# Two graph layers on one core: the product of two weight matrices moved to the front of the program, and the first batches planned anew

## The chip, the cores and the metric

The kernel runs on one core of a Trainium2 chip. The metric is the device time of one execution, in microseconds (us). The engines of a core are TensorE (PE, with its weight loads as PEld), VectorE (DVE), ScalarE (ACT), GpSimd (POOL) and SyncE (SP, which here only issues transfers). [...]

## The reference

There are 32 batches of a 512 x 512 matrix x, one 512 x 512 matrix adj for all of them, and weights of 512 x 512, all in float32. What is computed is this:

```
h = relu(layernorm(x))
x = x + (adj @ h) @ w0 + b0                     # layer 0
h = relu(layernorm(x))
q, k, v = h @ Wq + bq, h @ Wk + bk, h @ Wv + bv  # layer 1, 8 heads
scores = q @ k.T / 8 + (1 - adj) * -1e9
x = x + (softmax(scores) @ v) @ Wo + bo
```

The term with -1e9 makes the softmax of layer 1 pick, for each row of adj, the column with the largest entry, wherever that entry leads by enough. Then layer 1 is a gather of rows of h @ (Wv @ Wo) plus a constant row.

## The kernel before

**Front.** `gnn_two_layers` loads adj, x of batches 0 and 1, Wq, Wk and w0. It transposes adj on PE (L89) into `adjT` (copies at L104), makes the layer norm of batch 0 (`Norm`, with the power on POOL at L201 and the relu on ACT at L212), and multiplies it by adj (L139, called the aggregation; the result, transposed, is `yT`). Beside this DVE looks for the largest entry of each row of adj (L115 to L117), and PE counts which columns are used at all (`few`, L147, and `many`, L137 and L138). From these and from the sums of squares of Wq and Wk it makes a flag that says whether the gather is valid (L164, L165). All engines load the flag (L176) and branch. With these inputs they go to `single_path`; `general_path` is the full attention.

**The single path.** Its order is written by hand. For each batch number b, `todo` holds lists of functions for 21 steps; `put` files a function under a step. Three generators carry the PE work, and with each of their pieces one step's list is run before the piece's result is taken from PSUM. Steps 0 to 6 go with layer 0 of batch b, steps 7 to 13 with the aggregation of batch b+1, steps 14 to 20 with layer 1 of batch b-1. A 512 x 512 product is done in 7 pieces instead of 8 (`product`, matmuls at L288): p1, p5, u2, c11, c22, c12, c21. They use sums of blocks of both operands that DVE makes beforehand (`sum_a`, `sum_b`: `h0s`, `yTs` in the tile `sel`, `adjT_s`, `w0_t`, `wvo_t`, `hTs`). p1, u2, c22 and c21 accumulate in one bank, p5 and c12 in a second one, c11 in a third; a piece in a bank can begin only when the piece before it in that bank has been taken. Takes are copies on ACT or additions on DVE (L325, L327, L335, L338, L345).

**Batch 0.** It has no layer 1 of an earlier batch beside it. Layer 0 of batch 0 is done in plain rows (`layer0_rows`, L458), with DVE making the four `adjT_s` sums beside it. The aggregation of batch 1 follows; at its step 11 `number_rows` (L404 to L414) numbers the used rows with two small PE matmuls and ten small DVE operations, and the four `w0_t` sums are made. In place of layer 1, steps 14 to 20 run `fold_weights`: it transposes Wv (L364, copied by ACT at L365), multiplies it by Wo (L372, copied into `wvo` at L375), and sums the rows of bv-weighted Wo (`part`, made by `bias_part`; matmul L378) into the constant row `cvo` and its column form `cvo_c` (L381 to L385). wv, wo, bv and bo are loaded behind the branch (L587 to L589), ahead of the x of batch 2.

**Later batches.** `put_h` writes h of layer 1 by an indirect DMA in the order of the numbering, `get_h` fetches the used rows, `transpose_h` and `hT_sum` prepare them, layer 1 multiplies by `wvo`, and `finish` adds the gathered rows to x. For the last batch, layer 0 takes its pieces in the order p1, p5, u2, c22, c11, c12, c21, because no layer 1 lies between its aggregation and it.

Of the kernel before, what the change touches and what calls it, by code (L numbers as in the profile page):

```python
# [17 lines left out]
P = 128  # L18
# [7 lines left out]
def gnn_two_layers(ctx: ExitStack, tc: tile.TileContext, x, adj, w0, b0, wq, bq, wk, bk, wv, bv, wo, bo, out):  # L26
# [22 lines left out]
    def big(name):  # L49
# [3 lines left out]
    adjT, yT, w0_s, sel = big("adjT"), big("yT"), big("w0_s"), big("sel")  # L53
    wv_s, wo_s = xs[3], xs[4]
    b0_r = keep.tile([P, D], F32, name="b0_r")
# [7 lines left out]
    kept = dict(xs=xs, hs=hs, adjT=adjT, yT=yT, w0_s=w0_s, sel=sel, wv_s=wv_s, wo_s=wo_s, b0_r=b0_r, used=used,  # L63
                before=before, idx=idx, ident=ident, ones=ones, mhalf=mhalf)
# [3 lines left out]
    with ExitStack() as tmp, tc.manual_schedule():  # L68
# [4 lines left out]
        for c in range(C):  # L73
            nc.sync.dma_start(mask[:, c, :], adj[c * P:(c + 1) * P, :])
            nc.scalar.dma_start(xs[0][:, c, :], x[0, c * P:(c + 1) * P, :])
# [3 lines left out]
        wt = [look.tile([P, DC, D], F32, name=f"wt{i}") for i in range(2)]  # L79
        bt = [look.tile([P, DC], F32, name=f"bt{i}") for i in range(2)]  # L80

        def load_w(t, w):
            nc.scalar.dma_start(t, w.rearrange("(c p) o -> p c o", p=P))

        norms = [Norm(nc, small, mhalf, xs[0], hs[0], [0, 1]), Norm(nc, small, mhalf, xs[0], hs[0], [2, 3])]
        pts = [ps_l.tile([P, C, P], F32, name=f"pt{m}") for m in range(C)]
        for c in range(C):
            for m in range(C):
                nc.tensor.transpose(pts[m][:, c, :], mask[:, c, m * P:(m + 1) * P], ident)  # L89
            norms[c // 2].stats(c % 2)  # L90
            if c == 1:
                norms[0].power()
            if c == 2:
                norms[0].offset()
        norms[1].power()
        for t, v in zip(bt, (bq, bk)):
            nc.gpsimd.dma_start(t, v.rearrange("(c p) -> p c", p=P))
        nc.gpsimd.dma_start(b0_r, bass.AP(tensor=b0.tensor, offset=b0.offset, ap=[[0, P], [1, D]]))
        for i, w in enumerate((wq, wk)):
            norms[0].relu(i)  # L100
            load_w(wt[i], w)
        for m in range(C):
            eng = (nc.scalar.copy, nc.scalar.copy, nc.vector.tensor_copy, nc.vector.tensor_copy)[m]
            eng(adjT[:, m, :], pts[m].rearrange("p c q -> p (c q)"))  # L104
        norms[1].offset()
        for i in range(2):
            norms[1].relu(i)
        if B > 1:
            load_w(xs[1], x[1])
        load_w(w0_s, w0)  # L110

        sums = look.tile([P, 4], F32, name="sums")
        top = look.tile([P, C, 8], F32, name="top")
        for c in range(C):
            nc.vector.tensor_scalar(mask[:, c, :], mask[:, c, :], 1.0, NEG, op0=ALU.subtract, op1=ALU.mult)  # L115
            nc.vector.max(top[:, c, :], mask[:, c, :])
            nc.vector.tensor_scalar(sel[:, c, :], mask[:, c, :], top[:, c, 0:1], None, op0=ALU.is_equal)  # L117
        both = look.tile([P, N], F32, name="both")
# [6 lines left out]
        nc.vector.tensor_reduce(least, gap, AX.X, ALU.min)  # L125

        if B > 1:
            norms.append(Norm(nc, small, mhalf, xs[1], hs[1], range(C)))
            norms[2].stats(0)
            norms[2].stats(1)  # L130
        few = ps_l.tile([P, 4, C], F32, name="few")
        many = ps_l.tile([P, 4, C], F32, name="many")
        for d in range(DC):
            ps = ps_l.tile([P, N], F32, name="mm", bufs=2)
            for m in range(C):
                if d == 3 and m == 2:
                    nc.tensor.matmul(many[:, 0, :], ones, used, start=True, stop=True)  # L137
                    nc.tensor.matmul(many[:, 1, :], ones, sums, start=True, stop=True)  # L138
                nc.tensor.matmul(ps, hs[0][:, m, d * P:(d + 1) * P], adjT[:, m, :], start=(m == 0), stop=(m == C - 1))  # L139
# [5 lines left out]
            if d == 2:  # L145
# [3 lines left out]
                if B > 1:  # L149
                    norms[2].stats(2)  # L150
                    norms[2].stats(3)
                    norms[2].power()
        rows = look.tile([P, 1], F32, name="rows")
        nc.vector.tensor_reduce(rows, many[:, 0, :], AX.X, ALU.add)
        nc.vector.tensor_scalar(rows, rows, float(32 * S), None, op0=ALU.is_le)
# [7 lines left out]
        nc.vector.tensor_mul(sure, sure, rows)  # L163
        nc.tensor.matmul(few[0:1, 1, 0:1], sure, ones[:, 0:1], start=True, stop=True)  # L164
        nc.vector.tensor_copy(flag, few[0:1, 1, 0:1])  # L165
        if B > 1:
            norms[2].offset()
            for c in range(C):
                norms[2].relu(c)
# [9 lines left out]
    with cmp.Else():  # L179
        general_path(tc, x, adj, wq, bq, wk, bk, wv, bv, wo, bo, out, kept)  # L180

# [35 lines left out]
def single_path(ctx: ExitStack, tc: tile.TileContext, x, wv, bv, wo, bo, out, kept):  # L217
# [20 lines left out]
    xs, hs, adjT, yT, w0_s, sel, wv_s, wo_s, b0_r, used, before, idx, ident, ones, mhalf = (  # L238
        kept[k] for k in ("xs", "hs", "adjT", "yT", "w0_s", "sel", "wv_s", "wo_s", "b0_r", "used", "before", "idx",
                          "ident", "ones", "mhalf"))  # L240
# [15 lines left out]

    def blk(t, chunks, cols, half=HALF):
        return t[:, 2 * chunks:2 * chunks + 2, cols * half:(cols + 1) * half]

# [10 lines left out]

    def sum_b(s, t, i, half=HALF):
        b11, b12, b21, b22 = blk(t, 0, 0, half), blk(t, 0, 1, half), blk(t, 1, 0, half), blk(t, 1, 1, half)
        if i == 0:
            nc.vector.tensor_sub(s[:, 0], b12, b11)
        elif i == 1:
            nc.vector.tensor_sub(s[:, 1], b22, s[:, 0])
        elif i == 2:
            nc.vector.tensor_sub(s[:, 2], b22, b12)
        else:
            nc.vector.tensor_sub(s[:, 3], b21, s[:, 1])  # L280
# [68 lines left out]
    adjT_s, w0_t, wvo_t = (consts.tile([P, 4, 2, HALF], F32, name=n) for n in ("adjT_s", "w0_t", "wvo_t"))  # L349
    wvo = consts.tile([P, DC, D], F32, name="wvo")  # L350
    cvo = consts.tile([P, D], F32, name="cvo")
    cvo_c = consts.tile([P, DC], F32, name="cvo_c")
    bv_c = consts.tile([P, DC], F32, name="bv_c")
# [4 lines left out]
    wvT = work.tile([P, DC, D], F32, name="zs")  # L358

    def fold_weights():  # L360
        for j in range(DC):
            pt = ps_t.tile([P, DC, P], F32, name="pt")
            for i in range(DC):
                nc.tensor.transpose(pt[:, i, :], wv_s[:, i, j * P:(j + 1) * P], ident)  # L364
            nc.scalar.copy(wvT[:, j, :], pt.rearrange("p c q -> p (c q)"))  # L365
            if j % 2 == 1:
                for f in (yield) or ():
                    f()
        for i in range(DC):
            ps = ps_m.tile([P, D], F32, name="mm")  # L370
            for j in range(DC):
                nc.tensor.matmul(ps, wvT[:, j, i * P:(i + 1) * P], wo_s[:, j, :], start=(j == 0), stop=(j == DC - 1))  # L372
            for f in (yield) or ():
                f()
            nc.scalar.copy(wvo[:, i, :].rearrange("p (c q e) -> p q c e", q=4, c=4),  # L375
                           ps.rearrange("p (q c e) -> p q c e", q=4, c=4))
        ps = ps_m.tile([P, D], F32, name="mm")
        nc.tensor.matmul(ps, ones, part, start=True, stop=True)  # L378
        for f in (yield) or ():
            f()  # L380
# [5 lines left out]

    part = work.tile([P, D], F32, name="part")

    def bias_part(j):
        if j == 0:  # L390
# [556 lines left out]
```

## Time and profile before

| what | us |
|---|---|
| median of 3 runs | 1108.0 (1107.43 to 1109.12) |
| the profiled execution | 1104.05 |
| its span | 1101.6 |

The profile of one execution shows each engine's instructions with start and length. For a reader of this change the stages ahead of the third batch matter. This is how they lie in the profiled execution, read from PE's instructions in order of time:

| stage | PE from, to (us) |
|---|---|
| transposes of adj, as it comes in | 4.37 to 9.6 |
| aggregation of batch 0, counts, flag | 10.95 to 28.3 |
| layer 0 of batch 0, in rows | 29.63 to 43.44 |
| aggregation of batch 1, with the numbering | 43.44 to 57.35 |
| weights: transposes, product, sum of rows | 57.35 to 74.25 |
| layer 0 of batch 1 | 74.25 to 86.58 |
| aggregation of batch 2 | 86.58 to 98.67 |
| layer 1 of batch 0 | 98.67 to 107.31 |

In the lines of the trace, the columns are start, length (of the group, when several instructions are merged into a line), engine, source line, operation, output and inputs, shape, count, and in brackets the idle time of the engine before it with what ended it. A float32 matmul is carried out as two instructions, so 16 matmuls are shown as x32; a transpose is one instruction.

### The profile page before, as it was taken

How to read it: one execution, taken by the hardware profiler on the slowest of the kernel's cores; microseconds unless marked ns; L12 is line 12 of the kernel's file. 1: busy time of each engine (PE TensorE's matmuls, PEld its weight loads, DVE VectorE, ACT ScalarE, POOL GpSimd, SP SyncE). 2: the span in 40 equal slices, each digit the busy share in tenths (PEclk: the TensorE clock that was granted, in tenths of full speed). 3: DMA queues.
4: the chain of work that ended last, by engine and by line, in shares of the span. 5: the costliest groups of instructions: out<-in, count | busy, mean ns of one | idle time of the engine just before them, and what ended most of it. 6: DMA issues, size and time to landing. Idle time of an engine off the chain costs nothing.

```text
span 1101.6 us, 15852 instructions
## 1 busy us (share of the span) xinstructions
PE 1079.9 (98%) x5404; PEld 953.2 (87%) x5404; DVE 907.3 (82%) x1853; ACT 358.6 (33%) x655; POOL 443.8 (40%) x491
## 2 busy tenths in 40 slices
PE   7999999999999999999999999999999999999996
PEld 3569989999989989988999998999999899999883
DVE  6869888888888888878888888888888878888863
ACT  3223323233323333322323332323332232333221
POOL 2124544333554343454333454433355434345413
PEclk9999999999999999999999999999999999999999
DMA  6362676667777667767666776666776766676537
GB/s 238 125 141 74 172 191 148 160 175 197 182 181 158 149 171 193 187 171 169 157 156 189 193 189 177 146 160 173 196 179 181 164 149 171 184 193 155 141 105 245
DMA packets 162412, 186.90 MB, mean 170 GB/s; under 512 B 14993, under 2 KB 102289, under 8 KB 162321
## 3 DMA queue, kind: packets, MB, share of 16 engines
q1 hardware_dynamic: 130672, 112.70, 37.3%
q0 software_dynamic: 27968, 66.61, 27.0%
q10 hardware_dynamic: 3680, 6.49, 1.7%
q8 instruction: 44, 0.72, 0.3%
q14 instruction: 48, 0.39, 0.2%
HBM read 96.28 MB, written 89.46 MB: 169 GB/s over the span
## 4 chain that ended last, share of the span: by engine, by line
PE 94%; DMA 1%; DVE 1%; ACT 1%; POOL 1%; issue 1%; ACTq 0%; SPq 0%; POOLq 0%; DVEq 0%
PE mm L288 89%; PE mm L139 1%; PE mm L458 1%; PE mm L372 1%; PE mm L508 1%; POOL x L544 1%; DMA x<-in_x_dram 1%; DMA yT<-z,place 1%; ACT h L212 0%; DMA z<-zr 0%; DVE x L345 0%; DVE st L194 0%; ACT zs L338 0%; POOL yT L553 0%; DVE zr L535 0%
## 5 line engine op out<-in xcount | busy, mean ns | idle before, releaser
L544 POOL DMA_INDIRECT x<-z,place x116 | 182.8, 1576 | 370.6 <-DMA z<-zr 318.7
L327 ACT COPY yT<-mm 128x512 f32<-128x512 f32 x124 | 71.8, 579 | 562.0 <-PE mm L288 527.9
L345 DVE TENSOR_TENSOR x<-mm,x 128x512 f32<-128x512 f32 x217 | 149.7, 690 | 86.2 <-PE mm L288 86.2
L212 ACT ACTIVATE h<-x,off,rstd 128x512 f32<-128x512 f32 x256 | 194.9, 808 | 36.2 <-DVE off L204 34.2
L201 POOL TENSOR_TENSOR rstd<-ve,mhalf 128x2 f32<-128x2 f32 (+1 forms) x97 | 106.0, 1093 | 222.1 <-DVE ve L200 222.1
L194 DVE BATCH_NORM_STATS2 st<-x 128x6 f32<-128x512 f32 x256 | 171.5, 670 | 9.2 <-DMA x<-in_x_dram 8.0
L288 PE MATMUL mm<-w_t,sel 128*128 128x256 f32 x744 | 171.1, 380 | 0.8 <-DVE x L345 0.8
L288 PE MATMUL mm<-adjT_s,h0s 128*128 128x256 f32 x744 | 170.8, 380 | 1.0 <-ACT yT L327 1.0
L288 PEld LDWEIGHTS mm<-w_t,sel 128*128 128x128 f32 x744 | 141.5, 191 | 20.4 <-DVE x L345 1.6
L288 PEld LDWEIGHTS mm<-adjT_s,h0s 128*128 128x128 f32 x744 | 141.6, 191 | 20.2 <-ACT yT L327 1.4
L470 POOL DMA_INDIRECT hs<-h,dest x124 | 133.7, 1078 | 30.8 <-issue 22.2
L338 ACT ACTIVATE zs<-mm,cvo_c 128x176 f32<-128x176 f32 x248 | 87.2, 403 | 98.2 <-PE mm L288 98.2
L288 PE MATMUL mm<-hTs,wvo_t 128*128 128x176 f32 x720 | 117.5, 313 | 0.6 <-ACT zs L338 0.6
L288 PE MATMUL mm<-adjT,h 128*128 128x256 f32 x496 | 117.2, 380 | 0.0
L288 PE MATMUL mm<-w_s,yT 128*128 128x256 f32 x496 | 117.2, 380 | 0.0
L288 PEld LDWEIGHTS mm<-hTs,wvo_t 128*128 128x128 f32 x720 | 109.8, 191 | 1.1 <-ACT zs L338 1.1
L288 PEld LDWEIGHTS mm<-adjT,h 128*128 128x128 f32 x496 | 94.5, 191 | 13.0 <-issue 0.5
L288 PEld LDWEIGHTS mm<-w_s,yT 128*128 128x128 f32 x496 | 93.3, 191 | 11.5 <-issue 0.5
L436 DVE TENSOR_TENSOR x<-x,b_r 128x512 f32<-128x512 f32 x128 | 86.6, 678 | 0.0
L288 PE MATMUL mm<-hT,wvo 128*128 128x176 f32 x480 | 81.4, 313 | 0.0
L288 PEld LDWEIGHTS mm<-hT,wvo 128*128 128x128 f32 x480 | 75.3, 190 | 1.5
L325 DVE TENSOR_TENSOR yT<-mm,yT 128x512 f32<-128x512 f32 x93 | 63.9, 687 | 5.8 <-PE mm L288 3.0
(146 smaller groups left out, 1278.9 us busy)
## 6 DMA issues: line engine op xcount, KB each, us to landing
out_dram<-x SPq DMA_DIRECT2D x124, 256.0 KB, 4.1
x<-in_x_dram SPq DMA_DIRECT2D x120, 256.0 KB, 5.5
hc<-hs SPq DMA_DIRECT2D x124, 176.0 KB, 3.8
z<-zr SPq DMA_DIRECT2D x120, 96.0 KB, 2.0
z<-zr SPq DMA_DIRECT2D x120, 80.0 KB, 1.9
hs<-h,dest POOLq DMA_INDIRECT x124, 5.9
x<-z,place POOLq DMA_INDIRECT x116, 5.8
x<-in_x_dram ACTq DMA_DIRECT2D x4, 256.0 KB, 5.3
```

Of the source, the lines that this page charges most:

```text
L139: nc.tensor.matmul(ps, hs[0][:, m, d * P:(d + 1) * P], adjT[:, m, :], start=(m == 0), stop=(m == C - 1))
L194: self.nc.vector.bn_stats(st, self.src[:, self.chunks[i], :])
L201: self.nc.gpsimd.tensor_tensor(self.rstd, ve, self.mhalf[:, 0:n], ALU.pow)
L212: self.nc.scalar.activation(dst, src, AF.Relu, bias=self.off[:, i:i + 1], scale=self.rstd[:, i:i + 1])
L288: nc.tensor.matmul(bank[:, m, 0:half], lhs[:, k, m * P:(m + 1) * P], rhs[:, k, :], start=(first and m == 0 and k == 0), stop=(k == 1), ski ...
L325: nc.vector.tensor_add(dst, bank, dst)
L327: nc.scalar.copy(dst, bank)
L338: nc.scalar.activation(dst[:, m, :], bank[:, m, :], AF.Identity, bias=cvo_c[:, 2 * i + m:2 * i + m + 1])
L345: nc.vector.tensor_add(dst, bank, dst)
L436: nc.vector.tensor_add(X[b][:, c, :], X[b][:, c, :], b0_r)
L470: stored = nc.gpsimd.indirect_dma_start(out=HS[b], out_offset=bass.IndirectOffsetOnAxis(ap=dest[:, i:i + 1], axis=0), in_=H1[b][:, i, :], ...
L544: nc.gpsimd.indirect_dma_start(out=X[b][:, c, :], out_offset=None, in_=Z[b], in_offset=bass.IndirectOffsetOnAxis(ap=place[:, c:c + 1], axi ...
```

## The change

The product Wv @ Wo moves from batch 0 of the single path to the very front, and everything that hangs on it is rearranged:

- wv and wo are loaded first (wv in two halves, one each on the queues of SP and ACT; wo in four chunks in turn). adj, x of batch 0, Wq, Wk, w0 and x of batch 1 follow on SP. bv, bq, bk and b0 are loaded by POOL at once. ACT runs a small relu before its first copy.
- The front then transposes Wv, makes the product and `part`, and transposes adj between the first rows of the product. The search of the largest entries (`peaks`) and the norm of batch 0 stand beside it.
- The four `adjT_s` sums are made ahead of the aggregation of batch 0 and the four `w0_t` sums within it, both ahead of the branch. The relu of batch 1 is ahead of the flag too.
- `few` comes after the second of the aggregation's four rows instead of the third, `many` one matmul earlier.
- In batch 0 of the single path, `number_rows` is at step 1, the statistics of layer 1 at steps 2, 3 and 7, `put_h` at 9 and 11, `get_h` at 16, the norm of batch 2 at 8 to 14. The weights' steps fall away: layer 0 of batch 1 follows its aggregation directly, with its pieces in the order of the last batch.
- What is left of the weights (the matmul with `part` and the constant row: `add_up`) goes to step 11 of batch number 1, beside the aggregation of batch 2. The `wvo_t` sums go from steps 4, 4, 5, 5 to 5, 5, 6, 6.
- `general_path` keeps its Wq, Wk and h in the new tiles; it does not run with these inputs.

The diff, cut to its core:

```diff
-        for c in range(C):
-            nc.sync.dma_start(mask[:, c, :], adj[c * P:(c + 1) * P, :])
-            nc.scalar.dma_start(xs[0][:, c, :], x[0, c * P:(c + 1) * P, :])
+        nc.sync.dma_start(wv_s[:, 0:2, :], rows(wv, 0, 2))
+        nc.scalar.dma_start(wv_s[:, 2:4, :], rows(wv, 2, 2))
+        for c in range(DC):
+            (nc.sync, nc.scalar)[c % 2].dma_start(wo_s[:, c:c + 1, :], rows(wo, c, 1))
+        for t, w in ((mask, adj), (xs[0], x[0])):
+            for c in (0, 2):
+                nc.sync.dma_start(t[:, c:c + 2, :], rows(w, c, 2))
+        for t, w in [(wt[0], wq), (wt[1], wk), (w0_s, w0)] + [(xs[1], x[1])] * (B > 1):
+            nc.sync.dma_start(t, rows(w, 0, C))
...
+        for t, v in ((bv_c, bv), (bt[0], bq), (bt[1], bk)):
             nc.gpsimd.dma_start(t, v.rearrange("(c p) -> p c", p=P))
...
+        nc.scalar.activation(first, ones[:, 0:1], AF.Relu)
+
+        def transposed(t, dst, engines):
+            pts = [ps_l.tile([P, C, P], F32, name=f"pt{m}") for m in range(C)]
+            for c in range(C):
+                for m in range(C):
+                    nc.tensor.transpose(pts[m][:, c, :], t[:, c, m * P:(m + 1) * P], ident)
+                if c % 2 == 1:
+                    yield
+            for m in range(C):
+                engines[m](dst[:, m, :], pts[m].rearrange("p c q -> p (c q)"))
+            yield
...
+        for _ in transposed(wv_s, wvT, (nc.scalar.copy, nc.scalar.copy, nc.vector.tensor_copy, nc.vector.tensor_copy)):
+            pass
+        for j in range(DC):
...
+                nc.vector.scalar_tensor_tensor(part, wo_s[:, j, :], bv_c[:, j:j + 1], part, op0=ALU.mult, op1=ALU.add)
+        flips = transposed(mask, adjT, (nc.scalar.copy,) * 4)
+        for i in range(DC):
+            ps = ps_l.tile([P, D], F32, name="mm", bufs=2)
+            for j in range(DC):
+                nc.tensor.matmul(ps, wvT[:, j, i * P:(i + 1) * P], wo_s[:, j, :], start=(j == 0), stop=(j == DC - 1))
+            if i == 0:
+                next(flips)
+                peaks(0)
+                peaks(1)
+            if i == 1:
+                next(flips)
...
+            nc.scalar.copy(wvo[:, i, :].rearrange("p (c q e) -> p q c e", q=4, c=4),
+                           ps.rearrange("p (q c e) -> p q c e", q=4, c=4))
...
+        for i in range(4):
+            sum_b(nc, adjT_s, adjT, i)
...
-                if d == 3 and m == 2:
+                if d == 3 and m == 1:
                     nc.tensor.matmul(many[:, 0, :], ones, used, start=True, stop=True)
...
-            if d == 2:
+            if d == 1:
                 for m in range(C):
                     nc.tensor.matmul(few[:, 0, m:m + 1], both[:, m * P:(m + 1) * P], ones[:, 0:1], start=True, stop=True)
                 nc.vector.tensor_scalar_min(used, few[:, 0, :], 1.0)
...
+                    for c in range(C):
+                        norms[2].stats(c)
                     norms[2].power()
...
+                for i in range(4):
+                    sum_b(nc, w0_t, w0_s, i)
+                if B > 1:
+                    norms[2].offset()
+            if d == 2 and B > 1:
+                for c in range(C):
+                    norms[2].relu(c)
...
-        for t, w in ((wv_s, wv), (wo_s, wo)):
-            nc.sync.dma_start(t, w.rearrange("(c p) o -> p c o", p=P))
...
     def layer0(b):
-        if b == B - 1:
+        if b in (1, B - 1):
             return product(yT, yTs, w0_s, w0_t, take_onto(X[b]), pieces=("p1", "p5", "u2", "c22", "c11", "c12", "c21"))
...
+            if b == 0:
+                put(0, 1, lambda b: number_rows())
+                todo[3] += todo[4] + todo[5] + todo[6]
+                run(layer0_rows(0), todo[0:4])
...
+                put(1, 11, lambda b: add_up())
...
-            if b == 0:
-                run(fold_weights(), todo[14:21])
-            else:
-                run(layer1(b - 1) if b < B and b != B - 2 else None, todo[14:21])
+            run(layer1(b - 1) if 0 < b < B and b != B - 2 else None, todo[14:21])
```

`add_up` is the end of `fold_weights` (L378 to L385), unchanged. `sum_b` is the function of the same name in the single path, moved out of it.

## Prediction

> **What bounds the kernel now.** I read the page first: the engines' busy time, the slices and the chain that ended last.
>
> ```profile
> PE 1079.9 (98%) x5404; PEld 953.2 (87%) x5404; DVE 907.3 (82%) x1853; ACT 358.6 (33%) x655; POOL 443.8 (40%) x491
> PE   7999999999999999999999999999999999999996
> PE 94%; DMA 1%; DVE 1%; ACT 1%; POOL 1%; issue 1%; ACTq 0%; SPq 0%; POOLq 0%; DVEq 0%
> ```
>
> TensorE (PE) has work in every slice and carries 94% of the chain. So only three things can move the time: when PE starts, what it waits for, and how fast it is clocked. The edits touch the front and batches 0 and 1. From layer 0 of batch 2 on (107.31 us, the first L288 `w_s,yT` matmul after layer 1 of batch 0) the plan is the same but for the batch number in conditions. I therefore compare what lies ahead of 107.31. Next I read PE and its weight loads in order of time.
>
> ```profile
> 4.37 2.24 PE L89 MATMUL pt<-ident,mask 128*128 128x128 f32 x8 [4.37 <-DMA mask<-in_adj_dram]
> 8.50 1.12 PE L89 MATMUL pt<-ident,mask 128*128 128x128 f32 x4 [0.17 <-DMA mask<-in_adj_dram]
> 10.95 12.50 PE L139 MATMUL mm<-adjT,h 128*128 128x512 f32 x24 [1.33 <-ACT adjT L104]
> ...
> 13.67 0.34 PEld L139 LDWEIGHTS mm<-adjT,h 128*128 128x128 f32 x1 [0.52 <-issue]
> 14.52 0.34 PEld L139 LDWEIGHTS mm<-adjT,h 128*128 128x128 f32 x1 [0.52 <-issue]
> 15.13 0.19 PEld L139 LDWEIGHTS mm<-adjT,h 128*128 128x128 f32 x1 [0.27 <-issue]
> 15.56 0.19 PEld L139 LDWEIGHTS mm<-adjT,h 128*128 128x128 f32 x1 [0.24 <-issue]
> ```
>
> Dense work starts at 10.95. Its loads step by 0.85 us until about 14.95 and by 0.43 us afterwards: 4.0 us at half rate, 2.0 us lost. The page's PEclk row reads 9 throughout, so the spacing is the evidence. Then what PE waits for later, in order of time, and one row of the table by stage (busy us of PE, weight loads, DVE, ACT, POOL; clock; DMA):
>
> ```profile
> 55.52 2.00 PE L288 MATMUL mm<-adjT_s,h 128*128 128x256 f32 x8 [1.11 <-DVE yT L325]
> 57.35 1.04 PE L364 MATMUL pt<-ident,x 128*128 128x128 f32 x8
> 58.68 1.15 PE L364 MATMUL pt<-ident,x 128*128 128x128 f32 x8 [0.29 <-ACT zs L365]
> 59.66 13.90 PE L372 MATMUL mm<-x,zs 128*128 128x512 f32 x32
> 73.39 1.02 PE L378 MATMUL mm<-part,ones 128*128 128x512 f32 x2
> ...
> 1050.60 2.00 PE L288 MATMUL mm<-w_t,sel 128*128 128x256 f32 x8 [0.78 <-DVE x L345]
> ...
> 98.67:107.31 8.64, 8.63 (x58) 8.36 (x57) 8.54 (x20) 5.49 (x11) 3.85 (x4) 1.00 0.43 86
> ```
>
> The first row is `number_rows`: its VectorE (DVE) chain sat ahead of c22's take, and c21 accumulates in the bank that take reads. The row at 1050.60 is the one layer 0 that already runs in the order p1, p5, u2, c22. In the last row the third busy figure is DVE: 8.54 of 8.64 us in layer 1 of batch 0, no slack.
>
> **The change, part by part.**
>
> *Start of dense work.* Before, four adj and four x loads of 256 KB come in side by side; the fourth of the eight lands at 5.64, the last at about 8.8. Then relu and the adjT copies lead to 10.95. Now wv comes first, two 512 KB loads on two queues: the same first megabyte, so 5.6. Sixteen transposes at 0.28 (2.24 for 8) end at 10.1. The first copy (0.57, ACT) starts when its bank is done, three transposes earlier, and is over by then; wo, the second megabyte, is in by 8.8. The product starts at 10.1: **-0.85**. ACT's table load (1.28) is called early and leaves the path. Four ACT-queue issues of 0.39 to 0.52 (L83) go to SP, which has nothing else to do. The bias loads take 0.8 to 1.2 each of POOL from 1.6 on and land 6.5 to 7.6 after issue, so bv is there by 9.5; DVE wants it at 11.1.
>
> *Transposes.* Those of wv leave 57.35 to 59.66 (2.31 with the 0.29 wait); those of adj now stand between products at 16 x 0.13 = 2.08: **-0.23**. The weight product (13.73) only moves. Its sums and copies hide under it.
>
> *The clock.* [...] 4.5 us of transposes between 4.37 and 9.62 did not shorten the 4.0 us. But they had idle time among and behind them (0.60, 0.17, 1.33), which the new ones lack[...]. Ends 0 and -2.0; I take **-0.8**.
>
> *Ahead of the flag.* Eight sums and the four steps of `part` move here on DVE. Between the end of `few` (after the second row of products) and the flag, DVE has used 0.1, four stats 3.3, sums of w0 2.6, offset and count 1.2: 7.2 us. PE has two rows of products and `many`: 6.87 + 0.34 = 7.2. A tie: 0 (up to +0.5). Earlier the sums of adj and `both` end some 5 us ahead of need. x1 is the last of 8 MB at 0.3 to 0.37 MB/us, in by 32; its stats start at 36. ACT's four relus now stand ahead of the last yT copy and wait for the offset, so the copy ends about 2.4 us after PE's last row; PE needs it 1.45 (branch) + 2.58 (three steps) after: **0**, and +0.9 if PE waits for the whole of yT.
>
> *Behind the branch, batch 0.* Four adj sums (2.6) leave DVE there, numbering (1.6) and three stats enter; it stays about as full as the 13.74 of 13.81 that its stage shows. The numbering waits for PE's counts while the next row runs, so the yT wait goes: c21 came 3.09 after c12 and should come 1.73 after: **-1.36**. Next in line is the u bank: two relus at step 7 precede p1's ACT copy, due about 17.5 after the stage's start, u2 at 17.6: **+0.1** (0 to 1). Four indirect stores (some 1.3 each with the memset) move ahead on POOL, in front of batch 2's power; its offset then holds DVE some 0.5 us at step 12, with 2 us in hand before layer 0's p5. x2's load no longer queues behind 2 MB of weights on SP.
>
> *Layer 0 of batch 1* takes the order of 1050.60, whose rows show c22 waiting 0.78 (0.86 by starts): **+0.85**. The cvo chain (74.45 to 76.51 on DVE) leaves it, and with it the 0.24 by which this stage (12.33) exceeds the 12.1 of a later one: **-0.24**.
>
> *`add_up`.* Its matmul (0.86) only moves. Its DVE chain, 0.73 + 0.73 + 0.60 = 2.06 us, now stands at step 11 of batch 2's aggregation, ahead of c22's take, exactly where the numbering hurt. After c22: matmul 0.86, chain 2.06, take 0.69, 3.7 in all; c21 is due after 0.86 + 1.73 = 2.59: **+1.2**. Behind that, DVE starts layer 1 of batch 0 late. From one c22 take to the next it has 10.5 us of work without a gap; the take then ends about 22.1 us after the aggregation began, c21 is due at 21.25, and before it waited 0.2: **+0.6** (0 to 0.9).
>
> **Sum.** Without the clock: -0.85 - 0.23 - 1.36 + 0.1 + 0.85 - 0.24 + 1.2 + 0.6 = +0.07. With it: -0.7. The profiled execution took 1104.05 (span 1101.6 and 2.45 around it), so it would become 1103.3. It lies 4 us under the median of the runs, 1108.0, and the rows cannot say where the other runs lose that; I carry the difference over: **1107.3 us**. Two waits go, and three of the same kind come. A measurement of this kernel tells about 0.2%, 2.2 us, from no change.
>
> **Rivals.**
>
> *The clock comes up with the transposes.* Full -2.0 in place of -0.8, and the bank waits a little shorter than priced (each rests on ties of some tenths): -2.5 to -3.5, **1105.0**. For it: PE has no gap from 5.6 on. [...] Chance 0.28.
>
> *DVE's backlog doesn't bite.* If layer 0 of batch 1, with only 9.9 us of DVE work in 12.9, lets DVE enter the aggregation early enough, or the chain is overlapped, the 1.2 and 0.6 shrink to 0.3 or less: -2.2 to -2.6, **1105.6**. Against it: the chain can't begin before its own matmul, whatever DVE's lead. Chance 0.14.
>
> *The weights land late (slower).* PE's first work hangs on all of wv. If the first two megabytes share the 16 engines so that wv lands only with wo, at 8.6 in place of 5.6, all behind it moves by 3.0: +2.3, **1110.3**. It decides from a landing at about 8.5 on. For it: wo's four loads are queued at once, and three bias loads of single elements enter at the same time. Against it: within a queue the loads of before landed in order, over a microsecond apart. Chance 0.08.
>
> That the main case reaches over +2.2 by its own upper ends (u bank 1.0, yT 0.9, flag 0.5, clock 0) has 0.03; the trade itself 0.47. So faster 0.42, same 0.47, slower 0.11. The range, 1103.9 to 1109.8, takes in both faster rivals and the unknown costs of the main case.
>
> **What would show it.** The first `wv_s` transpose at 5.6 and the first product at 10.1; the place where load spacing falls to 0.43; no wait at the flag's matmul (L164); c21 of batch 1's aggregation 1.73 after c12; 0.78 at c22 of layer 0 of batch 1; some 1.2 at c21 of batch 2's aggregation, and more than 0.2 at the next c21. Wrong if layer 0 of batch 2 starts earlier than 105 or later than 109.

## The result, and the profile after

| | median of the runs (us) | ratio to before |
|---|---|---|
| before | 1108.44 (1107.43 to 1109.12, 4 runs) | |
| after | 1103.69 (1101.85 to 1104.13, 4 runs) | 0.9955 [0.9938, 0.9972] |

The change gains 4.75 us, just beyond the end of the range (1103.9). The profiled execution of after took 1104.13 with a span of 1102.3. The one of before had taken 1104.05 with 1101.6. So profile against profile nothing was gained, and run against run 0.45%. This contradiction is what the experiments are about.

The page of after, in the rows that were shown of before:

```profile
PE 1078.6 (98%) x5404; PEld 951.1 (86%) x5404; DVE 910.2 (83%) x1853; ACT 359.6 (33%) x656; POOL 437.8 (40%) x491
PE   7999999999999999999999999999999999999996
PE 90%; DVE 1%; DMA 1%; POOL 1%; issue 1%; ACT 1%; SPq 0%; POOLq 0%; DVEq 0%; ACTq 0%
```

The bound is the same. Now PE of after in order of time, with two of its weight loads from the same view:

```profile
5.80 3.32 PE L106 MATMUL pt<-ident,x 128*128 128x128 f32 x16 [5.80 <-DMA x<-in_L_gnn_Wv_dram]
9.47 3.70 PE L132 MATMUL mm<-x,yT 128*128 128x512 f32 x8 [0.35 <-ACT yT L110]
...
10.00 0.19 PEld L132 LDWEIGHTS mm<-x,yT 128*128 128x128 f32 x1 [0.24 <-ACT yT L110]
10.43 0.19 PEld L132 LDWEIGHTS mm<-x,yT 128*128 128x128 f32 x1 [0.24 <-issue]
...
42.61 8.80 PE L474 MATMUL mm<-w_s,yT 128*128 128x512 f32 x16 [2.19 <-ACT yT L182]
76.85 1.99 PE L333 MATMUL mm<-w_t,sel 128*128 128x256 f32 x8 [0.78 <-DVE x L390]
96.34 1.99 PE L333 MATMUL mm<-adjT_s,h 128*128 128x256 f32 x8 [1.10 <-DVE yT L370]
102.15 1.46 PE L333 MATMUL mm<-hTs,wvo_t 128*128 128x176 f32 x8 [1.42 <-ACT zs L383]
```

The loads are 0.43 us apart from the start: dense work begins warm, that is, at full clock. (Where the granted clock is 0.50 in this execution, from 44 to 46, they are 0.85 apart; at 1.00, from 48 on, 0.43.) The wait at c21 of batch 1's aggregation (55.52 of before) is gone. Four others have come: 2.19 at the first row product, 0.78 at c22, 1.10 at c21 of batch 2's aggregation, 1.42 at u2 of layer 1 of batch 0. The first costs more than its idle time. Windows of 2 us of the same execution (busy time of PE, weight loads, DVE, ACT and POOL, then the granted clock, DMA share and GB/s):

```profile
42.00:44.00 2.00, 1.39 (x2) 0.68 (x3) 2.00 (x7) 0.51 (x2) 0.00 (x0) 0.70 0.70 255
44.00:46.00 2.00, 2.00 (x4) 0.68 (x3) 1.81 (x4) 0.00 (x0) 0.60 (x1) 0.50 0.76 271
46.00:48.00 2.00, 2.00 (x6) 1.04 (x5) 0.12 (x1) 0.00 (x0) 0.00 (x0) 0.95 0.47 127
```

Behind the wait the clock is at half until about 46. The first 16 instructions of the row products take 8.80 us, the next 16 take 7.11, so 1.7 us are lost besides the wait.

### The profile page after: what moved, and what is told of

Read it like the earlier page. It is cut to its first block, busy times and chain, and to the rows that moved or that the text cites. A ratio compares the mean times of both kernels' runs of the same rounds, so it can differ in the third digit from the quotient of the medians.

```text
span 1102.3 us, 15852 instructions
## 1 busy us (share of the span) xinstructions
PE 1078.6 (98%) x5404; PEld 951.1 (86%) x5404; DVE 910.2 (83%) x1853; ACT 359.6 (33%) x656; POOL 437.8 (40%) x491
## 4 chain that ended last, share of the span: by engine, by line
PE 90%; DVE 1%; DMA 1%; POOL 1%; issue 1%; ACT 1%; SPq 0%; POOLq 0%; DVEq 0%; ACTq 0%
PE mm L333 89%; PE mm L474 1%; DMA yT<-z,place 1%; POOL x L560 1%; DVE x L390 0%; SPq L556 0%; POOL yT L569 0%; ACT h L272 0%; DMA z<-zr 0%; ACT zs L383 0%; DMA z<-hc 0%; DVE zs L380 0%; DVE zr L551 0%; DVE st L254 0%; ACT yT L372 0%
## 5 line engine op out<-in xcount | busy, mean ns | idle before, releaser
L486 POOL DMA_INDIRECT hs<-h,dest x124 | 126.7, 1022 | 23.7 <-issue 22.4
```

Of the source, the lines that this page charges most:

```text
L486: stored = nc.gpsimd.indirect_dma_start(out=HS[b], out_offset=bass.IndirectOffsetOnAxis(ap=dest[:, i:i + 1], axis=0), in_=H1[b][:, i, :], ...
```

## Experiments

The experiments ran on five chips, each with runs of the kernel before beside them. The kernel before took 1108.1, 1108.9 and 1108.6 us on the first, second and fourth, and 1104.0 and 1104.4 on the third and fifth; compare within a chip. "Layer 0 of batch 2 starts" is the mark of the prediction: 107.31 in the first profile of before, 108.44 in that of after.

**Both kernels again (chip 1).** No edit.

> The kernel before, unchanged, profiled once more and timed against itself. Theory A (the execution profiled first was a lucky one, with an early warm-up of TensorE's clock; the other executions lose some 4 us, and lose them ahead of 30 us by a later warm-up): a new profile shows a span of 1104 to 1107, and the load spacing falls to 0.43 later than 14.95, by up to twice the time lost. Theory B (the 4 us are lost somewhere in the long middle, by a clock below full or by single stalls): the front is as in the first profile and the third batch begins near 107.3 again, with the loss behind it. Theory C (the chip or the session differs): the new runs lie at 1104 like the first profile. Ratio to the kernel before 1.000 in each case.

> The changed kernel, unchanged, profiled once more. Its runs so far lie at 1101.9 to 1104.1. Theory A: warm by 7 to 11 us in every execution, since TensorE works without a break from 5.8 on; ratio 0.994 to 0.997. Theory B or C: the ratio depends on the session and can be nearer to 1.000. The wait of 1.4 us at u2 of layer 1 of batch 0 (102.15 in the first profile), which nothing in the plan explains, comes again if it belongs to the program and not if it was an accident.

Measured: before 1108.01 (22 runs), ratio 1.0004 [0.9998, 1.0011]; after 1103.25 (6 runs), 0.9956 [0.9944, 0.9968]. The profile of this execution of before (time 1107.17) is 3.1 us above the first one, and the front is not the reason: rows start at 30.05 instead of 29.63. The loss is in layer 1 of batch 0. First ACT there, then three windows of PE alone (busy, clock, DMA share, GB/s):

```profile
100.57 0.59 ACT L327 COPY yT<-mm 128x512 f32<-128x512 f32 x1 [6.18 <-PE mm L288]
103.55 1.30 ACT L338 ACTIVATE zs<-mm,cvo_c 128x176 f32<-128x176 f32 x4 [2.40 <-remote]
```

```profile
102.00:104.00 2.00, 0.00 (x0) 1.00 0.91 152
104.00:106.00 2.00, 1.69 (x7) 0.71 0.04 9
106.00:108.00 2.00, 2.00 (x8) 0.50 0.00 0
```

ACT takes p1 at 103.55. In the first profile of before it did so at 100.13:

```profile
100.13 0.70 ACT L338 ACTIVATE zs<-mm,cvo_c 128x176 f32<-128x176 f32 x2 [0.67 <-PE mm L288]
```

 "remote" is a release that the trace can't place. PE has no work for 2.67 us, and then runs at half clock (0.50 from 106 to 108). Layer 0 of batch 2 starts near 112.1 instead of 107.31. The profile on which I had predicted is one without this stall. Its 1104.05 lies below every timed run of before on the first, second and fourth chip (the lowest is 1104.83), and in the middle of those on the third and fifth (1102.1 to 1106.1). On which chip it was taken is not on record.

**Is it a late fetch of ACT's instructions? (chip 2)** 24 tiny copies on ACT at the start of the single path move its later instructions in the stream.

```diff
+        pad = small.tile([P, 1], F32, name="pad")
+        for _ in range(24):
+            nc.scalar.copy(pad, ident[:, 0:1])
```

> The kernel before with 24 small copies more on ScalarE at the start of the single path, where ScalarE is idle from 31.7 to 45 us; nothing reads them. In the second profile of the kernel before, ScalarE was late twice in layer 1 of batch 0 (the copy of c21 at 100.57, due at 99.3, and p1's take at 103.55, due at 100.5); TensorE waited 2.67 us there, its clock then stood at half for 3.5 us, and that makes the 4 us between the first profile and the usual time. Theory A (ScalarE's instructions arrive late at that place of its stream, since a block of them is fetched too late): the 24 copies move the place earlier in the stream, to steps with slack; the wait at layer 1 of batch 0 goes and the median falls from 1108 to about 1104. Theory B (the late start comes from what happens around it in time: the small gathers, traffic, a semaphore): the copies change nothing, 1108.

Measured: 1107.12, ratio 0.9988 [0.9978, 0.9997]; the take of p1 still waits 3.54 for "remote" and PE 2.53. This way of moving it does not remove the stall. The traces speak against a late fetch too: in none of the eight profiles that show the stall (of both kernels and their variants) does a packet of an instruction queue move in the last 3.3 us before the late take. In this one the next lands between 106 and 107, after the take at 104.46.

**Is it GpSimd's small gathers? (chips 2, 4 and 5)** In that stretch POOL issues the four gathers of row places (`look_up`, one 4-byte entry per row).

```diff
-                put(1, 11, lambda b: look_up(tables[0]))
+                put(1, 18, lambda b: look_up(tables[0]))
```

> The kernel before with the four small gathers of the table (look_up) at step 18 of batch 1 instead of step 11. Theory A (late instructions): no change, 1108, and the wait of 2.7 us stays at p1's take of layer 1 of batch 0. Theory B (GpSimd's gathers of 4-byte elements delay ScalarE): the wait goes or shrinks below 1 us, and the median falls by 2 to 4 us.

> The kernel before, unchanged, on the same chip as the kernel after. In the first profile of before and in a variant of it with a quicker front, ScalarE's take of p1 in layer 1 of batch 0 was on time (0.7 us after the end of p1), in another profile 2.4 us late. Theory: what the change gains hangs on that stall. Where the stall is there, before takes about 1108 and the kernel after 0.4% less; where it isn't, before takes about 1104 and the ratio of the kernel after is between 0.998 and 1.001. Rival: the gain lies elsewhere, and the ratio of the kernel after is 0.995 to 0.997 with the stall or without.

> The kernel after, unchanged. Theory: about 1103.3 with the same three waits as in its first profile (2.19 at the first row product of layer 0 of batch 0, 0.78 at c22 of layer 0 of batch 1, 1.10 at c21 of the aggregation of batch 2); its wait of 1.42 at u2 of layer 1 of batch 0 is there only where the kernel before stalls too, and is otherwise under 0.3, then at about 1102. Rival: the wait at u2 is there in any case, as the order of its VectorE work makes it.

> The kernel before with the four gathers at step 18 of batch 1, as in the run before it on another chip (ratio 0.9972). Theory: it gains only by the stall: ratio 0.997 where the kernel before stalls; 0.999 to 1.001 where it doesn't. Rival: the gathers cost the same on every chip: 0.997 either way.

Measured: on chip 2 the moved gathers give 1106.08, ratio 0.9972 [0.9962, 0.9982]. On chip 4 before (as `f_before`) takes 1108.41, after 1103.79 (0.9962 [0.9948, 0.9977]), and before with the gathers moved 1104.44 (0.9969 [0.9957, 0.998]). This one edit gains nearly what the whole change gains. PE, ACT and POOL of before on chip 4, and then ACT of before with the gathers moved:

```profile
103.63 2.52 PE L288 MATMUL mm<-hTs,wvo_t 128*128 128x176 f32 x8 [2.53 <-ACT zs L338]
...
102.87 1.30 ACT L338 ACTIVATE zs<-mm,cvo_c 128x176 f32<-128x176 f32 x4 [3.53 <-remote]
...
100.56 1.04 POOL L423 DMA_INDIRECT place<-table,idx  x1 [0.30 <-issue]
```

```profile
98.24 0.59 ACT L327 COPY yT<-mm 128x512 f32<-128x512 f32 x1 [4.90 <-PE mm L288]
99.49 0.70 ACT L338 ACTIVATE zs<-mm,cvo_c 128x176 f32<-128x176 f32 x2 [0.67 <-PE mm L288]
```

With the gathers moved, the take follows the copy after 0.67. With them in place the take starts 1.27 after the last gather's issue ends (102.87 against 101.60). In after on chip 4 the lag is 1.50 (101.42 against 99.92), on chip 1 it is 1.41 before and 1.56 after. The stall ends shortly after the gathers.

Moving them brings another wait, though. In all four profiles of before with the gathers moved, PE waits 1.04 or 1.05 at c21 of the same stage, because the power of the norm on GpSimd (`rstd`) takes 3.22 us instead of the 1.41 or 1.42 in the five with the gathers in place, and DVE waits for it (0.94 on chip 4). On chip 4:

```profile
101.47 3.22 POOL L201 TENSOR_TENSOR rstd<-ve,mhalf 128x4 f32<-128x4 f32 x1 [5.61 <-DVE ve L200]
...
106.41 1.46 PE L288 MATMUL mm<-hTs,wvo 128*128 128x176 f32 x8 [1.05 <-DVE zs L335]
```

So the stage takes 9.67 there, 3.2 less than with the stall and 1.0 more than the 8.64 of the first profile.

What the stall costs differs. In before, layer 1 of batch 0 takes 12.83 us on chip 4 (98.55 to 111.38), against 8.64 without the stall: 4.2 more. In after it takes 9.99 (98.26 to 108.25). There the gathers' last issue ends 1.66 after the stage's start instead of 3.05, so PE waits 1.37 instead of 2.53, and no drop of the clock follows (u2's 8 instructions take 1.46, in before 2.52).

**Does the gain hang on the stall? (chip 5)** Both kernels, each with and without the gathers moved.

> The kernel after, unchanged, beside the same kernel with its gathers moved. Where the kernel before takes about 1108 on this chip: 1103.5 with a wait of 1.4 at u2 of layer 1 of batch 0. Where the kernel before takes about 1104: the same without that wait, about 1102.5, a ratio of 0.998 to 1.000. The rival, that the gain does not hang on the stall, gives 0.995 to 0.997 in both cases.

> The kernel after with the gathers at step 18. Theory: the gathers hold ScalarE's take of p1 here too, and without them the wait at u2 goes: 0.8 to 1.4 us below the kernel after on a chip where its wait of 1.4 is there, the same within 0.4 us where it isn't. Rival: what is taken away at u2 comes back at c21 of the same stage, where the addition of c12 by VectorE was 0.6 us late with the gathers moved: no gain on either.

> The kernel before with the gathers at step 18, as base for the change without the stall. Theory: with the stall out of both, the change is worth next to nothing, as the sum of the prediction had it: the kernel after with its gathers moved is between 1.3 us quicker and 0.5 us slower than this one. Rival: the change gains 3 us or more without the stall as well.

On this chip before takes 1104.38 (41 runs), and after 1103.77: ratio 0.9998 [0.999, 1.0007]. With the gathers moved, after takes 1103.87 (0.9998 [0.999, 1.0007]) and before 1104.99 (1.0007 [0.9999, 1.0016]). So where before takes 1104, the change is worth nothing that can be measured, and moving the gathers helps neither kernel. That before doesn't stall on this chip is read from its time; there is no trace of it on this chip. After takes 1103.3 to 1103.8 on every chip where it ran. PE, ACT, POOL and DVE of after here:

```profile
43.77 7.10 PE L474 MATMUL mm<-w_s,yT 128*128 128x512 f32 x16 [2.20 <-ACT yT L182]
106.60 1.46 PE L333 MATMUL mm<-hTs,wvo 128*128 128x176 f32 x8 [1.64 <-DVE zs L380]
...
99.03 0.71 ACT L383 ACTIVATE zs<-mm,cvo_c 128x176 f32<-128x176 f32 x2 [0.61 <-PE mm L333]
...
101.66 3.21 POOL L261 TENSOR_TENSOR rstd<-ve,mhalf 128x4 f32<-128x4 f32 x1 [2.38 <-DVE ve L260]
...
104.91 0.16 DVE L264 SCALAR_TENSOR_TENSOR off<-mv,rstd 128x4 f32<-128x4 f32 x1 [0.93 <-POOL rstd L261]
```

The take of p1 is on time and the wait at u2 is gone, but c21 of the same stage now waits 1.64 for DVE, and DVE has waited 0.93 for GpSimd's power. Layer 1 of batch 0 then depends on two things, which the profiles of after show in all four combinations (us of the stage):

| after | power 3.21 us | power 1.41 us |
|---|---|---|
| ScalarE's take late | 10.27 (first profile; 10.26 on chip 1) | 9.99 (chip 4) |
| take on time | 10.26 (chip 5) | 9.24 (gathers moved, chip 3) |

So the stall costs after 0 to 0.75 us, where it costs before 4.2: c21 has to wait for DVE anyway, and the clock doesn't drop (1.00 over this stage in the first profile of after). This is why the same kernel is nearly equally fast on both kinds of chip, and before is not. Why the power takes 3.2 us in some executions and 1.4 in others no run says; both occur with the gathers in place and with them moved. The first expectation's 1102.5 left the wait at c21 out.

**The gathers moved in after (chip 3).** The same edit.

> The kernel after, with the four gathers of row places issued at step 18 of batch 1 instead of step 11; nothing else. Theory: GpSimd's small gathers hold up ScalarE's work while they are in flight, in the kernel after as in the one before: the copy of p1 in layer 1 of batch 0 is then on time (within 0.5 us of the end of p1), TensorE's wait of 1.42 us at u2 goes, and the time falls by 1.0 to 2.0 us, to about 1101.8. Rival: the wait at u2 in the kernel after comes from the backlog on VectorE and the power on GpSimd ahead of it, as the prediction had it: the wait stays at 1 us or more and the time stays at 1103.3.

Measured: 1103.34, ratio 0.9997 [0.9989, 1.0006] to a before of 1103.98. The wait at u2 is gone, and the time is that of after elsewhere. In this profile the power is short, and 0.62 at c21 is left:

```profile
103.12 1.40 POOL L261 TENSOR_TENSOR rstd<-ve,mhalf 128x4 f32<-128x4 f32 x1 [7.33 <-DVE ve L260]
...
107.04 1.46 PE L333 MATMUL mm<-hTs,wvo 128*128 128x176 f32 x8 [0.62 <-DVE zs L380]
```

The stage takes 9.24, which is 0.60 more than in the first profile of before.

**Do transposes lift the clock? (chips 3 and 5)** Before, with 16 transposes more, whose result is not used, around those of adj.

```diff
+        warm = ps_l.tile([P, N], F32, name="mm", bufs=2)
         for c in range(C):
+            for _ in range((9, 0, 2, 0)[c]):
+                nc.tensor.transpose(warm[:, 0:P], ident, ident)
...
+        for _ in range(5):
+            nc.tensor.transpose(warm[:, 0:P], ident, ident)
```

> The kernel before, with 16 more transposes of the identity into a spare bank: nine ahead of the first transpose of adj, two in the middle and five behind the last, so that TensorE does nothing but transposes from about 2 us to the first dense product. Their result is not used. Theory: transposes lift the clock as any product does: the weight loads of the dense work are 0.43 us apart from the first one on (0.85 before, until about 15 us), the flag's product comes some 2 us earlier, and the time falls by 1.5 to 2.5 us. Rival (transposes don't count, and the quicker start of the kernel after has another cause): [...]the time stays within 0.5 us of the kernel before.

> The kernel before with the gathers at step 18 and with 16 more transposes of the identity around those of adj, whose result is not used: the clock's part of the change alone, with the stall out of it. Theory: transposes count as work for the clock[...]: full at about 12 us instead of 15 to 16; 0.8 to 1.6 us below the kernel with the gathers alone. Rival: within 0.4 us of it, the quicker front being caught up by VectorE's work ahead of the flag.

The first weight loads of dense work with the extra transposes, chip 3:

```profile
9.03 1.08 PEld L99 LDWEIGHTS mm<-ident 128*128 128x128 f32 x5
10.40 0.50 PEld L144 LDWEIGHTS mm<-adjT,h 128*128 128x128 f32 x2 [0.29 <-ACT adjT L109]
11.42 0.34 PEld L144 LDWEIGHTS mm<-adjT,h 128*128 128x128 f32 x1 [0.52 <-ACT adjT L109]
12.08 0.19 PEld L144 LDWEIGHTS mm<-adjT,h 128*128 128x128 f32 x1 [0.33 <-issue]
12.51 0.19 PEld L144 LDWEIGHTS mm<-adjT,h 128*128 128x128 f32 x1 [0.24 <-ACT h L217]
```

Full clock comes at about 12.0 instead of 15.0 (before's first profile) or 16.2 (its second). That is 1.7 us into dense work, which began at 10.40. Before needed 4.0 us of dense work in its first profile (from 10.95) and 5.6 in its second (from 10.59). With more transposes ahead the full clock comes sooner: they count. The flag's product comes at 26.96 instead of 28.15, and layer 0 of batch 2 starts at 106.10 instead of 107.31. On chip 5, with the gathers moved in both, it is 107.16 instead of 108.70. The times show less: 1103.19, ratio 0.9993 [0.9985, 1.0002] on chip 3; 1104.48 against 1104.99 on chip 5, with intervals that touch. So the effect is shown in the trace, at 1.2 to 1.5 us in these kernels, and not resolved in the time. The expected 2 us were too much. On chip 5 dense work is at full clock from its start at 10.38 (7.13 us for its first 16 instructions), 1.7 us earlier than on chip 3, and the flag's product still comes at 26.96, because PE now waits for ScalarE's copy of yT (0.30 at the same place on chip 3):

```profile
18.56 3.70 PE L144 MATMUL mm<-adjT,h 128*128 128x512 f32 x8 [1.04 <-ACT yT L147]
```

That the clock would come up at about 12, as expected there, was wrong as well.

**The new waits of after, one by one.**

The four relus of batch 1 behind the last copy of yT (chip 2):

```diff
-            if d == 2 and B > 1:
+            if d == 3 and B > 1:
```

> The changed kernel with ScalarE's four relus of batch 1 behind the last copy of yT instead of ahead of it. In both profiles of the changed kernel TensorE waits for that copy behind the branch (42.61 and 42.97, 2.39 us after the flag's matmul, where before it was 1.48), and the clock stands at half for the next 3.5 us. Theory: the wait falls to 1.4, the clock stays up, layer 0 of batch 0 takes 14.2 us instead of 15.95: -2.7 us, 1100.5. Rival (the clock drops for the 1.4 us too, or the relus are late for the sums of h0): -0.9 or less.

Measured: 1101.74, ratio 0.9932 [0.9917, 0.9947]. In the first profile of after ACT ran the four relus from 39.11 on and began the copy, which stands behind them in the program, at 41.95. The wait ahead of the rows is 1.22 instead of 2.19 and the clock stays full (7.10 for the first 16 instructions of the rows). By stages that is 2.7 us: 0.97 of the wait and 1.69 of the clock. Layer 0 of batch 2 starts at 106.98 instead of 108.79 (after on chip 1), only 1.8 earlier, since in this profile PE waits 0.93 for the first half of adj, until 14.18. (Three others of after's variants wait 0.36 to 0.67 there.)

`add_up` at step 3 of batch number 1 instead of 11 (chip 2):

> The changed kernel with add_up at step 3 of batch 1 (layer 0) instead of step 11 (aggregation). By the first profile c21 of the aggregation waits 1.10 us behind add_up's chain on VectorE. At step 3 three pieces lie between the take that the chain delays and the piece that needs it. Theory: that wait goes and no other comes, -1.1 us at least; if the late p1 take of layer 1 of batch 0 (a wait of 1.42 us) is VectorE's backlog too, it goes as well, -2.5 in all. If it is ScalarE's late instructions, it stays or grows by the 1.1 us gained. Rival (the chain delays c22's take and so c21 of layer 0): 0.

Measured: 1104.55, 0.9962 [0.9947, 0.9977]. The wait at c21 goes, but the norm on DVE is later, ACT's relus and copy with it, and u2 of the same aggregation waits 1.16 instead. The wait at u2 of layer 1 of batch 0 grows from 1.42 to 2.10. Nothing is gained.

Layer 0 of batch number 1 in the standard order (chip 3):

```diff
-        if b in (1, B - 1):
+        if b == B - 1:
```

> The kernel after, with layer 0 of batch 1 in the standard order of pieces (c11 ahead of c22), as in the kernel before; nothing else. Theory: the wait of 0.78 us at c22 goes and the stage takes 12.3 us instead of 13.14; the time falls by 0.6 to 0.9 us. Rival: the addition of c22 comes later in this order, what follows on VectorE is later too, and the aggregation of batch 2 waits by as much more: the time stays within 0.3 us of the kernel after.

Measured: 1102.32, 0.9985 [0.9977, 0.9992], which is 1.0 under after with the gathers moved on the same chip (1103.34). The 0.78 at c22 is gone.

The relus, the gathers and the order together (chip 3):

> The kernel after with three edits together: the relus of batch 1 behind the last copy of yT, the gathers of row places at step 18, and layer 0 of batch 1 in the standard order. If the three costs are independent: 1.6 for the relus as measured alone, about 1.4 for the gathers and 0.8 for the order, so 1099.5, in a range of 1098.5 to 1100.5. If two of the waits stand one behind the other on the same path: 1101 to 1101.7, no better than the relus alone.

Measured: 1099.8, 0.9958 [0.9944, 0.9971] to a before that has no stall. That is 3.5 under after with the gathers moved on the same chip; the relus and the order add, with 2.7 and 1.05 by their stages (layer 0 of batch 1 takes 12.09 in the standard order instead of 13.14).

And with `add_up` taken apart over steps 1 to 3 (chip 4):

```diff
-                put(1, 11, lambda b: add_up())
+                for i in range(3):
+                    put(1, 1 + i, lambda b, i: add_up(i), i)
```

> The kernel with relus behind the last copy of yT, gathers at step 18 and the standard order in layer 0 of batch 1, and with add_up besides taken apart over steps 1 to 3 of batch 1 (product and addition, product with the identity, sum), where VectorE has four idle stretches of 0.44 us. Theory: the wait of 1.10 us at c21 of the aggregation of batch 2 goes and nothing comes in its place: 1098.7, a ratio of 0.4% below the kernel after. Rival, as when add_up was moved alone: VectorE's norm comes later, ScalarE's copies in the aggregation of batch 2 come late, and the time is that of the three edits, 0.3% below the kernel after.

Measured: 1098.26, ratio 0.9915 [0.99, 0.993]; 5.5 us under after on the same chip (1103.79). Of PE's waits between the flag and layer 0 of batch 2 these are left in the trace:

```profile
42.37 7.11 PE L476 MATMUL mm<-w_s,yT 128*128 128x512 f32 x16 [1.22 <-ACT h L272]
101.98 1.46 PE L333 MATMUL mm<-hTs,wvo 128*128 128x176 f32 x8 [0.61 <-DVE zs L380]
```

This version beats both kernels.

## Why the prediction was wrong

**The step that failed** is the last of the sum: "It lies 4 us under the median of the runs, 1108.0, and the rows cannot say where the other runs lose that; I carry the difference over: **1107.3 us**". The sum itself had said 1103.3 for the profiled execution, and after takes 1103.3 to 1103.8. The 4 us were no constant. They are one stall, in a stage that I had priced, and the profile at hand happened not to have it. In before it costs 4.2 us (2.5 of waiting and the clock behind it). In after it falls on a stage that waits for DVE anyway, and costs 0 to 0.75. On chip 4 layer 0 of batch 2 starts 3.1 us earlier in after than in before, and 0.7 more are saved outside the span; the rest of the 4.6 between the medians is no more than single profiles differ by (what lies behind that mark takes 992.6 to 994.5 us in those of both kernels). On chip 5, where before takes 1104, the forecast of "same" would have been right (0.9998).

That the sum's 1103.3 came so near is partly luck. Ahead of layer 0 of batch 2 the change lost 1.13 us against the first profile, where the sum had -0.7. Of this 0.43 came back behind that mark and 0.62 outside the span, which I had taken as unchanged.

The terms of the sum, measured between the two first profiles (by starts on PE):

| term | predicted | measured |
|---|---|---|
| start of dense work | -0.85 | -1.48: the transposes took 0.21 each, not 0.28; then PE waited 0.35 for a copy (10.95 to 9.47) |
| clock | -0.8 (0 to -2.0) | -2.0: warm from the first product (up to 1.1 less in other profiles of after and its variants) |
| wait for the whole of yT | 0 (to +0.9) | +0.9 (2.39 from flag to rows, 1.48 before), and +1.7 of clock that follows it |
| numbering and u bank | -1.26 | -1.39 (aggregation of batch 1: 13.91 to 12.16; 0.36 of the difference are the numbering's two products, which only moved to the rows) |
| transposes | -0.23 | -0.45 (weights and transposes together: 16.04 to 15.59) |
| layer 0 of batch 1, order and cvo | +0.61 | +0.81 (12.33 to 13.14) |
| `add_up` | +1.2 | +1.36 (12.09 to 14.31, without its matmul of 0.86) |
| DVE backlog, layer 1 of batch 0 | +0.6 | +1.63 (8.64 to 10.27): 0.60 of backlog, and 1.0 by GpSimd's long power |

They add to +1.1; layer 0 of batch 2 starts 1.13 later. Each wait that the prediction named is at its place. Most sizes held; these did not:

- *The clock*: the -0.8 was my estimate between the two ends, and nothing at hand showed how transposes act on the clock. That those of before "did not shorten the 4.0 us" was not shown either: no run without them was there. Here transposes alone, from 5.80 to 9.12, left PE warm at 9.47 (loads 0.43 us apart), and the runs with extra transposes bear it out. From the start of work to the full clock it took 3.7 us or less here and some 5.9 in after on chip 5, where the first product's 8 instructions take 4.69 instead of 3.70. Why the two differ no run says.
- *The whole of yT*: I had both ends and took the wrong one. No end held the clock's return: an idle time of 2.2 us was priced at its length, and costs nearly twice that.
- *DVE's backlog*: the 0.6 was right where GpSimd's power took 1.4 us (9.24 against 8.64, chip 3). Where it took 3.2 us, 1.0 came on top. I had no term for it, since the power took 1.41 in the profile at hand.
- *Time outside the span*: I carried 2.45 over. It is 2.25 to 2.5 in all profiles of before and its variants, and 1.7 to 1.85 in all of after and its variants, so 0.6 to 0.7 of the gain lie there. No run says why; the extra transposes leave it at 2.4, the 24 copies on ScalarE at 2.25.

**The rivals.** The clock did come up with the transposes (full at 9.47, 0.35 us after their end), but the 2 us were spent on the wait (2.19) and the clock's return (1.7) ahead of the rows. The rival in which the backlog doesn't bite fell: `add_up` costs 1.36, and the backlog the 0.6 that was priced. The weights came in time (first transpose at 5.80, 5.6 predicted).

**What stays open.** Why ScalarE's take waits for GpSimd's gathers on three chips and not on two, and by what path. (On chips 3 and 5 the traces without it are those of after and of variants with the gathers at their old place.) That the gathers at their place are the cause is shown by moving them on two of the three; what releases ScalarE isn't in the trace. Why GpSimd's power takes 1.4 or 3.2 us is open too.

## What to carry to other kernels

Where the profiled execution is quicker than every timed run, the difference is itself a finding: take another profile and look for the stage that differs before it is carried over as a constant. A wait was worth more than its idle time where the clock dropped behind it (2.19 us and 1.7 more ahead of the rows of after), and less than that where the next engine in line was late anyway; so the same stall cost 4.2 us in one plan and at most 0.75 in the other. When work is moved, look at which copies and additions the moved instructions now stand in front of: removing the waits that the change had brought was worth 5.5 us on chip 4, more than the change itself.

## What the runs showed of the hardware

- An idle time of PE of 2.2 us ahead of the rows was followed by about 3.5 us of half clock in seven of eight profiles of after and its variants that have it; in one (chip 5) the clock stayed full (7.10 for those 16 instructions). After 2.5 and 2.7 us (before, layer 1 of batch 0) it dropped each of three times. It didn't after the one of 2.10 (`add_up` at step 3: granted clock 1.00 from 102 to 108), nor after 1.4. So the length of the idle time alone does not decide it here.
- The granted clock shows these later drops (0.50), but reads 1.00 through the cold start (10 to 16 us of before), where the loads are 0.85 us apart, twice the later 0.43.
- With four gathers of 128 entries of 4 bytes on GpSimd, ScalarE's take stood idle for up to 3.5 us and came 1.3 to 1.6 us after the end of the last one's issue in seven of eight profiles with the stall. In the eighth (`add_up` at step 3) it came 1.2 us after the third, and the next take 1.3 us after the fourth. The other twelve profiles have the take on time: eight with the gathers moved, three on chips 3 and 5, and the first of before.
- One power of 128x4 on GpSimd took 3.2 us in nine profiles and 1.3 to 1.4 in the others, at one place of the program only; elsewhere none took more than 1.41.
